# A four-layer graph network on one core: one transpose moved from TensorE to transfers and VectorE, and the last layer's side steps pinned to given units

## The chip, the cores and the metric

The kernel runs on one core of a Trainium2 chip. The engines are TensorE (PE, whose weight loads are listed as PEld), VectorE (DVE), ScalarE (ACT), GpSimd (POOL) and SyncE (SP), which here issues transfers between the device memory and SBUF. Each engine works through its own list of instructions in order and waits on semaphores. The metric is the device time of one execution in microseconds (us).

## The reference, cut to what matters

All values are float32. The input x holds 128 samples of 64 nodes with 256 features, and adj is one 64 by 64 adjacency matrix. Each of four layers adds a graph network's output to its input and normalises the result over the features.

```python
x = _layernorm(x + _L0_gnn_ref(x, adj, W, a))      # attention: softmax over masked scores, times x @ W
x = _layernorm(x + _L1_gnn_ref(x, ...))            # 4 heads, attention along 512 edges
x = _layernorm(x + _L2_gnn_ref(x, adj, ...))       # normalised adjacency, two linear maps, batch norms
x = _layernorm(x + _L3_gnn_ref(x, adj, ...))
...
def _L3_gnn_ref(x, adj, ...):
    h = relu(einsum('ts,bsh->bth', adj, x @ Wg0 + bg0))
    h = relu(einsum('ts,bsh->bth', adj, h @ Wg1 + bg1))
    for p in range(1, 5):                          # windows of p nodes through an LSTM
        nw = Tv // p
        wins = h[:, :nw * p, :].reshape(Bv * nw, p, Hd)
        last = _lstm_last(Wih[p - 1], Whh[p - 1], ..., wins)
        h = h.at[:, arange(nw) * p + (p - 1), :].set(last...)   # overwritten in place
    return h
```

So in the last layer every window length p reads what the one before has written.

## The kernel before, in words

**Recording.** A tile layer records the instructions, tracks which tile each reads and writes, and a scheduler then sets the order on every engine. `tc.issue_after(t)` makes what is recorded inside it stand behind instruction t on t's engine only; it adds no wait. A pool with `bufs=n` hands out n buffers in turn, and a new use waits for the last reader of the old one.

**Layers 0 and 1** go through the 8192 rows in 16 blocks called q, of 512 rows each, 128 on the partitions and four to a partition. For each q, `load_x` (L126) fetches the rows into `xin`; `l0_a` (L208) makes the transposed copy `tT` (features on the partitions) with `transposed` (L191): eight 128 by 128 TensorE transposes (L197) into two PSUM banks and two ScalarE copies (L198) out of them. `l0_b` multiplies it by the weights (L218), `l0_c` to `l0_e` do the attention, add the residual (L261) and write the normalised rows into `A[:, q, :]`. Layer 1 takes these, transposes them in the same way (`l1_t`), and `tT` has a single buffer that both use. The loop over q (its list of steps is at L649) interleaves: after each of eight `l1_graph` calls it runs the listed steps, among them `l0_e(q+1)` and `l0_a(q+2)` in the first slot and `l0_b(q+2)` in the third. `step` keeps TensorE's order as recorded; the other engines follow the scheduler. `load_x(q+2)` is called at the end of `l0_e(q)`. `A` has no other use for a q's columns before that, except that the setup keeps small tables in the columns at its upper end.

**The last layer** works on eight groups g of 16 samples. `lstm(g)` yields after each of 22 *units*: a unit computes the gates of one half (j) of the hidden state for one time step of one window length, with the input products on L970, the recurrent ones on L976, gate functions on L982 and L990, cell products on L985 to L989, and the new hidden state on L997 or L999. Units 0 to 3 belong to p=1, 4 to 7 to p=2, 8 to 13 to p=3, 14 to 21 to p=4. For p below 4 the last step overwrites `H` in place.

Between units, *side steps* are put in. `gcn(g, half)` makes the next group's H: it loads layer 2's residual (x2r), scales `A` (L879), transposes (by `turned`, in groups 1 to 7), adds (L884), normalises, then two graph products (L866, L909, L921, L866). `final(g, s)` transposes a quarter of the finished H, adds x3 (L1024), normalises and stores. `turned` (L844) is a transpose without TensorE: VectorE transposes squares of 32 (L848), one transfer writes the result to device memory (`way`, L851), four read it back with the squares in place (L853).

`steps_of(g)` gives the order of the 16 gcn steps of a group, and the loop hands them out evenly: after unit u, steps are run until done reaches (u+1)*16/20. `final(g, s)` runs whole after unit 14+2s, and the last one after unit 0 of the next group. Nothing there binds the order of ACT, DVE and POOL beyond the data.

```python
            while done < min(n_side, (u + 1) * n_side / (n_units - 2)):
                next(side, None)
                done += 1
```

Of the kernel before, what the change touches and what calls it, by code (L numbers as in the profile page):

```python
# [8 lines left out]
F32 = mybir.dt.float32  # L9
# [8 lines left out]
P = 128  # L18
NB = 128
N = 64  # L20
D = 256
KD = D // P
# [6 lines left out]
QT = 512  # L29
# [5 lines left out]
SKIP = 4  # L35
# [6 lines left out]
def kernel(ctx: ExitStack, tc: tile.TileContext, i, out):  # L42
    nc = tc.nc
# [68 lines left out]
    with ExitStack() as two:  # L112
# [13 lines left out]
        def load_x(q):  # L126
            xin[q] = xp.tile([P, PQ, D], F32, name="xin")
            nc.sync.dma_start(xin[q], x_view[q])

# [78 lines left out]
        def l0_a(q):  # L208
            L0[q] = {"x": xin.pop(q)}
            L0[q]["xT"] = transposed(L0[q]["x"], q)  # L210
# [611 lines left out]
    ST = 5  # L822
# [47 lines left out]
    def gcn(g, half, bank, name):  # L870

        q = g * 2 + half
        for a in range(2):
            x = work.tile([P, 2, D], F32, name="x2r", bufs=4)
            nc.sync.dma_start(x.rearrange("p c d -> p (c d)"), x2_dram[q][:, a * 2 * D:(a + 1) * 2 * D])
            blk = A[:, q, a * QT:(a + 1) * QT]
            z = blk.rearrange("p (c m t) -> p c m t", c=2, m=KD)
# [3 lines left out]
            if g:  # L881
                xt = turned(z.rearrange("p c m t -> p (c m) t"))
                xv = x.rearrange("p c (m i f) -> p c m i f", m=KD, f=32)
                nc.vector.tensor_add(xv, xt, xv)  # L884
            else:
                xt = bank([2, D])
                for m in range(KD):
                    for c in range(2):
                        nc.tensor.transpose(xt[:, c, m * P:(m + 1) * P], z[:, c, m, :], ident)
                nc.vector.tensor_add(x, xt, x)  # L890
            x3 = blk.rearrange("p (c d) -> p c d", c=2)
# [4 lines left out]
            yield  # L896
# [107 lines left out]
    def final(g, s, pieces=1):  # L1004
# [14 lines left out]
        o = work.tile([P, 2, D], F32, name="st", bufs=ST)  # L1019
        for cs in ([(0, 1)] if pieces == 1 else [(0,), (1,)]):  # L1020
            r = slice(cs[0], cs[-1] + 1)
            if pieces == 1:
                xv = xr.rearrange("p c (m i f) -> p c m i f", m=KD, f=32)
                nc.vector.tensor_add(xv, turned(h.rearrange("p c m t -> p (c m) t")), xv)  # L1024
            else:
                ht = gbank([2, D])
                for c in cs:
                    for k in range(KD):
                        nc.tensor.transpose(ht[:, c, k * P:(k + 1) * P], h[:, c, k], ident)
                nc.vector.tensor_add(xr[:, r], ht[:, r], xr[:, r])  # L1030
            layernorm(o[:, r], xr[:, r], len(cs), nc.gpsimd)
            for c in cs:
                nc.sync.dma_start(rows[1][c], o[:, c, :])

    def steps_of(g):

        if g:
            parts = [gcn(g, half, gbank, "hT") for half in range(2)]
            order = [0, 0, 1, 1] + [0] * (GCN_STEPS - 2) + [1] * (GCN_STEPS - 2)
        else:  # L1040
            parts = [gcn(g, 0, gbank, "hT"), gcn(g, 1, lbank, "hid")]
            order = [0, 0, 1, 1] + [0, 1] * (GCN_STEPS - 2)
        for half in order:
            next(parts[half])
            yield

    for _ in steps_of(0):
        pass
    n_units = sum(-(-(N // p) // (QT // GB)) * p * KD for p in range(1, SKIP + 1))
    first4 = n_units - SKIP * KD  # L1050
    for g in range(NG):

        side = steps_of(g + 1) if g + 1 < NG else iter(())
        n_side, done = 2 * GCN_STEPS, 0
        for u, _ in enumerate(lstm(g)):
            if u == 0 and g:
                final(g - 1, SKIP - 1)
            s, odd = divmod(u - first4, 2)
            if not odd and 0 <= s < SKIP - 1:
                final(g, s)  # L1060
            while done < min(n_side, (u + 1) * n_side / (n_units - 2)):
                next(side, None)
                done += 1
    final(NG - 1, SKIP - 1, pieces=2)
# [40 lines left out]
```

## Time and profile before

| | |
|---|---|
| median of 11 runs | 2175.81 us (2168.69 to 2177.08) |
| the profiled execution, its own time | 2176.67 us |
| its span, first to last instruction | 2174.9 us, mean granted TensorE clock 0.986 |
| PE / PEld busy | 2083.5 us (96%) / 1341.5 us (62%) |
| DVE / ACT / POOL busy | 863.4 us (40%) / 945.3 us (43%) / 415.8 us (19%) |
| transfers | 105.54 MB in 169275 packets, 86832 of them under 512 B |

Times in a view are counted from the start of the span. Layers 0 and 1 take about the first 560 us, layer 2 runs to about 850 us, and the last layer fills the rest. A row of a group of instructions reads: line, engine, operation, what is written and read, the shape, the count, then busy time and the mean of one, then the engine's idle time just before these instructions and what ended it. Matmuls overlap, so the time from one start to the next is the time that one costs; the printed duration is longer.

### The profile page before, as it was taken

How to read it: one execution, taken by the hardware profiler on the slowest of the kernel's cores; microseconds unless marked ns; L12 is line 12 of the kernel's file. 1: busy time of each engine (PE TensorE's matmuls, PEld its weight loads, DVE VectorE, ACT ScalarE, POOL GpSimd, SP SyncE). 2: the span in 40 equal slices, each digit the busy share in tenths (PEclk: the TensorE clock that was granted, in tenths of full speed). 3: DMA queues.
4: the chain of work that ended last, by engine and by line, in shares of the span. 5: the costliest groups of instructions: out<-in, count | busy, mean ns of one | idle time of the engine just before them, and what ended most of it. 6: DMA issues, size and time to landing. Idle time of an engine off the chain costs nothing.

```text
span 2174.9 us, 29437 instructions
## 1 busy us (share of the span) xinstructions
PE 2083.5 (96%) x11463; PEld 1341.5 (62%) x11463; DVE 863.4 (40%) x2054; ACT 945.3 (43%) x1825; POOL 415.8 (19%) x569
## 2 busy tenths in 40 slices
PE   6999999998999979999999999999999999999997
PEld 4667677775454434576576576477467468468466
DVE  7355655454544444134233333323323423423223
ACT  3766766674338153234234334333333333333332
POOL 1123333333210012011111111211211211202012
PEclk8999999999999989999999999999999999999999
DMA  3023222332221022012112111201201202201001
GB/s 124 20 42 52 45 49 50 53 51 42 42 86 59 0 87 78 0 47 67 42 35 63 58 30 58 69 21 52 85 10 59 87 6 60 72 1 59 20 7 52
DMA packets 169275, 105.54 MB, mean 49 GB/s; under 512 B 86832, under 2 KB 152368, under 8 KB 168880
## 3 DMA queue, kind: packets, MB, share of 16 engines
q1 hardware_dynamic: 167280, 101.70, 17.7%
q8 instruction: 90, 1.47, 0.3%
q0 software_dynamic: 1024, 1.05, 0.2%
q10 hardware_dynamic: 832, 0.92, 0.1%
q14 instruction: 49, 0.40, 0.1%
HBM read 59.59 MB, written 44.04 MB: 48 GB/s over the span
## 4 chain that ended last, share of the span: by engine, by line
PE 79%; DVE 7%; ACT 6%; DMA 3%; issue 2%; POOL 1%; SPq 1%; DVEq 0%; POOLq 0%; ACTq 0%
PE l L970 31%; PE l L976 19%; PE pz L707 5%; PE pz L772 4%; PE e L311 3%; PE g L909 2%; PE m L283 2%; PE g L921 2%; DMA way<-st 2%; PE m L218 2%; PE m L286 2%; PE g L866 1%; PE z L320 1%; PE m L401 1%; ACT A L879 1%
## 5 line engine op out<-in xcount | busy, mean ns | idle before, releaser
L970 PE MATMUL l<-H,wih 128*128 128x256 f32 (+2 forms) x2496 | 789.2, 471 | 9.9 <-ACT gate_g L990 4.4
L970 PEld LDWEIGHTS l<-H,wih 128*128 128x128 f32 x2496 | 469.9, 190 | 302.8 <-issue 189.2
L976 PE MATMUL l<-hid,whh 128*128 128x256 f32 (+2 forms) x1536 | 437.9, 438 | 2.4 <-DVE hid L999 2.4
L976 PEld LDWEIGHTS l<-hid,whh 128*128 128x128 f32 x1536 | 292.9, 191 | 131.7 <-issue 61.2
L982 ACT ACTIVATE gate_i<-l,bias 128x256 f32<-128x256 f32 (+2 forms) x176 | 100.0, 568 | 516.2 <-PE l L976 444.3
L985 DVE TENSOR_TENSOR gate_i<-gate_i,gate_g 128x256 f32<-128x256 f32 (+2 forms) x96 | 48.3, 503 | 432.8 <-ACT gate_g L982 432.7
L986 POOL TENSOR_TENSOR cell<-gate_f,cell 128x256 f32<-128x256 f32 (+2 forms) x96 | 84.5, 880 | 671.0 <-ACT gate_f L982 670.9
L83 POOL TENSOR_TENSOR ln_rs<-ln_rs,mhalf 128x2 f32<-128x2 f32 (+2 forms) x97 | 79.6, 821 | 688.0 <-DVE ln_rs L95 687.7
L322 ACT ACTIVATE u<-z 128x1024 f32<-128x1024 f32 x128 | 130.5, 1026 | 56.1 <-PE z L320 55.2
L982 ACT ACTIVATE gate_g<-l,bias 128x256 f32<-128x256 f32 (+2 forms) x176 | 100.2, 569 | 99.3 <-PE l L970 50.1
L990 ACT ACTIVATE gate_g<-cell 128x256 f32<-128x256 f32 (+2 forms) x176 | 90.0, 511 | 91.2 <-DVE cell L989 46.4
L982 ACT ACTIVATE gate_o<-l,bias 128x256 f32<-128x256 f32 (+2 forms) x176 | 99.2, 564 | 62.3 <-PE l L976 54.4
L707 PE MATMUL pz<-A,w 128*128 128x512 f32 x256 | 113.1, 595 | 0.0
L989 DVE TENSOR_TENSOR cell<-gate_i,gate_g 128x512 f32<-128x512 f32 (+2 forms) x80 | 49.9, 623 | 137.8 <-ACT gate_g L982 137.6
L294 DVE TENSOR_TENSOR qs<-m,qs 64x256 fp32r<-64x256 f32 x128 | 54.0, 422 | 121.8 <-ACT qs L293 120.1
L320 PE MATMUL z<-gath_r,qs 128*128 128x512 f32 x256 | 98.4, 472 | 0.0
L707 PEld LDWEIGHTS pz<-A,w 128*128 128x128 f32 x256 | 47.9, 190 | 55.3 <-issue 53.3
L283 PE MATMUL m<-wq,tT 128*128 128x260 f32 x256 | 72.5, 407 | 6.7 <-ACT yT L391 4.0
L982 ACT ACTIVATE gate_f<-l,bias 128x256 f32<-128x256 f32 (+2 forms) x96 | 51.0, 532 | 60.4 <-PE l L976 59.5
L999 DVE TENSOR_TENSOR hid<-gate_o,gate_g 128x256 f32<-128x256 f32 (+2 forms) x96 | 48.6, 507 | 67.8 <-ACT gate_g L990 39.8
L999 DVE TENSOR_TENSOR H<-gate_o,gate_g 128x512 f32<-128x512 f32 (+1 forms) x64 | 41.2, 643 | 80.3 <-PE l L970 68.0
L709 DVE BATCH_NORM_STATS2 st<-pz 128x6 f32<-128x512 f32 x64 | 44.4, 697 | 59.3 <-PE pz L707 59.2
(241 smaller groups left out, 2539.0 us busy)
## 6 DMA issues: line engine op xcount, KB each, us to landing
way<-st SPq DMA_DIRECT2D x59, 256.0 KB
st<-way SPq DMA_DIRECT2D x236, 64.0 KB
xin<-in_x SPq DMA_DIRECT2D x16, 512.0 KB
ld<-table SPq DMA_DIRECT2D x16, 512.0 KB
x_dram<-y SPq DMA_DIRECT2D x16, 512.0 KB
x2r<-x_dram SPq DMA_DIRECT2D x32, 256.0 KB
x_dram<-A SPq DMA_DIRECT2D x64, 128.0 KB
x3r<-x_dram SPq DMA_DIRECT2D x64, 128.0 KB
```

Of the source, the lines that this page charges most:

```text
L83: nc.gpsimd.tensor_tensor(dst, dst, mhalf[:, :n], OP.pow)
L283: nc.tensor.matmul(pq, xT[:, k, c * P:(c + 1) * P], wq[:, k, :], start=k == 0, stop=k == KD - 1)
L320: nc.tensor.matmul(z[:, k, :], L1[q]["qs"][c][:, s, k * P:(k + 1) * P], gath_r, start=True, stop=True)
L322: nc.scalar.activation(u, z, AF.Relu)
L707: nc.tensor.matmul(p_, w1[:, k, m * P:(m + 1) * P], A[:, q, k * QT:(k + 1) * QT], start=k == 0, stop=k == KD - 1)
L772: nc.tensor.matmul(p_, w2[:, k, m * P:(m + 1) * P], hidden(q, k), start=k == 0, stop=k == M1 - 1)
L970: nc.tensor.matmul(gates[n], wih[p][:, k, mw * P:(mw + 1) * P], Hw[:, k, :, s, :], start=k == 0, stop=not s and k == KD - 1)
L976: nc.tensor.matmul(gates[n], whh[p][:, k, m * P:(m + 1) * P], hid[:, k], start=False, stop=k == KD - 1)
L982: nc.scalar.activation(act[n], gates[n], AF.Tanh if n == "g" else AF.Sigmoid, bias=bias[:, p - 1, m:m + 1])
L986: nc.gpsimd.tensor_tensor(cell[:, j], act["f"], cell[:, j], OP.mult)
L990: nc.scalar.activation(act["g"], cell[:, j], AF.Tanh)
L999: nc.vector.tensor_mul(Hw[:, jj, :, s, :] if over else new[:, jj], o, t)
```

## The change

It has two parts.

**Layer 0.** For q from 1 on, `load_x` issues eight more transfers from SP. They read the same 512 rows again, and put 32 features' columns of every block of 32 rows on a quarter of the partitions, in pieces of 32 floats, into `A[:, q, :]`. `l0_a` then makes `tT` with one VectorE transpose of squares of 32 over 128 partitions by 1024 columns. The eight TensorE transposes and two ScalarE copies of these q are gone; q=0 is as before.

**Last layer.** `gcn`'s transposing half-steps are split for groups 1 to 7: two `fetch` steps (load, scale, turn) and two `norm` steps (add, normalise, store), so a half has ten steps. `final` is split at the turn's transfers into two steps, and takes its output tile only after the add. Each step is given a unit, in the tables AT and AT1 (a negative number counts back into the group before), in place of the even spread; steps on the same unit run with the later gcn steps first. All that a side step records on ACT, DVE and POOL stands behind the unit's last instruction there.

```diff
@@ load_x
             nc.sync.dma_start(xin[q], x_view[q])
+            if q:
+                rows = i["x"][q * QT:(q + 1) * QT, :].rearrange("(j t) (k i f) -> i k t j f", t=32, k=KD, f=32)
+                for n in range(4):
+                    for k in range(KD):
+                        to = A[n * 32:(n + 1) * 32, q, k * QT:(k + 1) * QT]
+                        nc.sync.dma_start(to.rearrange("t (j f) -> t j f", f=32), rows[n, k])
@@ l0_a
-            L0[q]["xT"] = transposed(L0[q]["x"], q)
+            if q:
+                L0[q]["xT"] = work.tile([P, KD, QT], F32, name="tT", bufs=1)
+                nc.vector.transpose(L0[q]["xT"].rearrange("p k t -> p (k t)"), A[:, q, :])
+            else:
+                L0[q]["xT"] = transposed(L0[q]["x"], q)
@@ gcn
-        for a in range(2):
+        def fetch(a):
             x = work.tile([P, 2, D], F32, name="x2r", bufs=4)
...
             if g:
-                xt = turned(z.rearrange("p c m t -> p (c m) t"))
...
+                return x, turned(z.rearrange("p c m t -> p (c m) t"))
...
+        def norm(a, x, xt):
+            xv = x.rearrange("p c (m i f) -> p c m i f", m=KD, f=32) if g else x
+            nc.vector.tensor_add(xv, xt, xv)
...
+        if g:
+            came = []
+            for a in range(2):
+                came.append(fetch(a))
+                yield
+            for a in range(2):
+                norm(a, *came[a])
+                yield
+        else:
+            for a in range(2):
+                norm(a, *fetch(a))
+                yield
@@ final
-        o = work.tile([P, 2, D], F32, name="st", bufs=ST)
...
+                ht = turned(h.rearrange("p c m t -> p (c m) t"))
+                yield
...
-                nc.vector.tensor_add(xv, turned(h.rearrange("p c m t -> p (c m) t")), xv)
+                nc.vector.tensor_add(xv, ht, xv)
...
+            o = work.tile([P, 2, D], F32, name="st", bufs=ST)
             layernorm(o[:, r], xr[:, r], len(cs), nc.gpsimd)
@@ the loop over groups
-    def steps_of(g):
...
+    AT = [[5, 5, 6, 6, 7, 9, 9, 13, 13, 15], [-7, -6, -4, -2, 1, 3, 3, 7, 7, 11]]
+    AT1 = [0, 0, 1, 2, 3, 5, 5, 7, 7, 11]
+    side = {}
+    for g in range(NG):
+        for half in range(2) if g else ():
+            part = gcn(g, half, gbank, "hT")
+            for n, u in enumerate(AT1 if half and g == 1 else AT[half]):
+                side.setdefault((g - 1) * n_units + u, []).append((n < 7, part))
+        for s in range(SKIP):
+            if g < NG - 1 or s < SKIP - 1:
+                part = final(g, s)
+                u = (g + 1) * n_units if s == SKIP - 1 else g * n_units + first4 + 2 * s
+                for v in (u, u + 1 + s // (SKIP - 1)):
+                    side.setdefault(v, []).append((True, part))
+    engines = (mybir.EngineType.Activation, mybir.EngineType.DVE, mybir.EngineType.Pool)
     for g in range(NG):
-        side = steps_of(g + 1) if g + 1 < NG else iter(())
-        n_side, done = 2 * GCN_STEPS, 0
         for u, _ in enumerate(lstm(g)):
-            if u == 0 and g:
-                final(g - 1, SKIP - 1)
...
+            traced = nc.cur_bb.bb.instructions
+            with ExitStack() as order:
+                for e in engines:
+                    order.enter_context(tc.issue_after([t for t in traced[-300:] if t.engine == e][-1]))
+                for _, part in sorted(side.pop(g * n_units + u, []), key=lambda t: t[0]):
+                    next(part)
```

## The prediction

> **What bounds the kernel now.** I read the busy table by stretches of time first, to see which engine each stage leans on, then the groups of instructions, then the chain of waits and the timeline around the places that the change touches. The busy table, in microseconds of each engine:
>
> ```profile
> core 0: us, PE busy (x) PEld busy (x) DVE busy (x) ACT busy (x) POOL busy (x), PEclk, DMA share, GB/s
> 300.00:400.00 100.00, 94.70 (x857) 68.24 (x855) 58.44 (x155) 66.37 (x146) 34.05 (x41) 1.00 0.28 53
> 1400.00:1600.00 200.00, 198.63 (x981) 129.67 (x980) 65.47 (x146) 70.64 (x129) 30.09 (x44) 1.00 0.14 43
> ```
>
> TensorE is nearly always busy in both stages, and VectorE, ScalarE and the transfers have room. So an edit pays if it takes TensorE work away (layer 0) or one of its few gaps (last layer). The groups concerned:
>
> ```profile
> L197 PE MATMUL m<-ident,xin 128*128 128x128 f32 x128 | 18.3, 288 | 8.0 <-DMA xin<-in_x 5.6 <-ACT spad L295 2.4
> L970 PE MATMUL l<-H,wih 128*128 128x512 f32 x770 | 338.2, 595 | 7.0 <-DVE H L999 3.7 <-ACT gate_g L990 3.4
> L976 PE MATMUL l<-hid,whh 128*128 128x256 f32 x768 | 175.5, 382 | 2.4 <-DVE hid L999 2.4
> ```
>
> The last two rows (between 860 and 2175 us) hold nearly all idle time of TensorE inside the LSTM: 9.4 us. The wait table counts 6 waits for H, 7 for gate_g and a single one for hid, so the first two recur once a group. Here is layer 0's place in the chain, and the group boundary from p=1 to p=2 on TensorE's and VectorE's timelines:
>
> ```profile
> 297.80 1.02 ACT u L322
> 298.83 0.03 issue
> 298.85 0.18 ACT spad L295
> 299.03 0.04 issue
> 299.07 1.09 PE m L197 x8
> 300.16 0.47 PE z L320 x2
> ```
> ```profile
> 1189.50 2.81 PE L970 MATMUL l<-H,wih 128*128 128x512 f32 x6 [0.48 <-ACT gate_g L990]
> 1192.88 1.55 PE L970 MATMUL l<-H,wih 128*128 128x512 f32 x3 [0.56 <-DVE H L999]
> ```
> ```profile
> 1188.67 0.68 DVE L999 TENSOR_TENSOR H<-gate_o,gate_g 128x512 f32<-128x512 f32 x1
> 1191.53 0.69 DVE L884 TENSOR_TENSOR x2r<-st,x2r 128x512 f32<-128x512 f32 x1 [2.18 <-DMA st<-way]
> 1192.13 0.69 DVE L999 TENSOR_TENSOR H<-gate_o,gate_g 128x512 f32<-128x512 f32 x1
> ```
>
> The eight transposes stand in the chain, behind a PSUM bank that ScalarE frees. At 1189 TensorE, with no side step in its list, waits for the first half of H; then VectorE's second H product stands behind an add (L884) whose transfer lands late, though its input was there by 1190. The end of the kernel has the same fault once, with a final's add in front:
>
> ```profile
> 2145.73 3.26 DMA st<-way
> 2149.12 0.70 DVE x3r L1024
> 2151.09 0.34 DVE gate_i L985
> 2152.48 0.44 DVE hid L999
> ```
>
> [...]the 512-column ones last 595 ns but start 429 ns apart, so I count starts. [...]the new ones have 128 B. The trace has their like: the table loads (ld<-table, 4096 pieces of 128 B each) took 21.7 ns a piece on one of 16 engines, against some 50 ns for 1024 B, so four times the cost per byte.[...] the turns here show 1.9 to 3.9 us. [...]the 128x512 transposes took 690 to 708 ns[...].
>
> **Layer 0, step by step.**
> *Removed:* 15 times eight transposes. Their starts are 109 ns apart, so 0.87 us for each q; also two ScalarE copies of 597 ns. In the chain above, the next matmuls (L320) could start when ScalarE's u is done, 298.83, instead of 300.16: 1.3 us. I take 1.0 us for each of the 14 q in the loop, 14.0 us, with ends 0.87 and 1.3.
> *Added on VectorE:* 15 transposes of 128x1024, which the trace lacks. [...]at most twice 708 ns, 1.42. In the changed order each stands between two of the qs subtractions (L294), just after the matmuls that release tT. There VectorE waits for ScalarE: L294 has 121.8 us of idle time before its 128 instructions. tT is then ready near 298, and its reader L218 comes at 303.85, or 302.5 without the transposes. So it costs nothing[...].
> *Added transfers:* 120 issues on SP. The xin issue takes 0.37 us, the ld ones with eight times as many pieces 0.5 to 3.1; at 0.4 to 0.5 that is up to 60 us of SP. 61440 pieces of 21.7 ns are 83 us of all 16 engines. Neither is near a limit: the order puts them right behind the xin loads, far ahead of use, most within the first 280 us, and the DMA share there goes from about 0.25 to about 0.55. Queued behind them on SP are the next xin, ld<-table and y stores. Each batch has eight transfers, 5.5 us, and the next ld waits for the scatters anyway. A late ld would hold POOL at L379, whose product L387 reads 11 us later (278.75 to 289.94). xin itself is now needed only for the residual.
> *q=1 in the setup:* its transpose comes behind L497 (23.77), so L218 starts near 26 instead of 23.52. ScalarE, which slowed L218 there, is free by then, and VectorE idles 4.04 us before L261: +0.5 us, between 0 and 2.5.
>
> **Last layer, step by step.** Matmuls, turns and adds are the same in number; they are moved.
> *p=1 to p=2:* the changed order puts the two L909 products (eight matmuls, 8 x 0.43 = 3.4 us) right after unit 3, and no x2r add there. TensorE now works while both H products are made (needed: 0.7 us for the first, some 2 for the second). Gone is, start to start, 1189.50 - (1184.56 + 10 x 0.429) = 0.65 and 1192.88 - (1189.50 + 6 x 0.429) = 0.81, about 0.73 over the groups. Groups 1 to 6: 6 x 1.38 = 8.3 us. Group 7 has no side step and keeps its 0.65.
> *The end:* the changed VectorE order puts the last final's add behind the hid product that it held up: 2.4 us gone. The add then waits in front of a unit about 13 us later than the turn, which takes about 9.
> *New waits:* half 0's adds stand at unit 6, one unit (13.7 us at p=2) behind the fetches; two turns on SP take about 15, but its VectorE products end 3 us after the unit. Its L866 comes 17 us after unit 6's end (unit 7 and the L921 products), the norms need about 8.5. Final's add stands one unit (2.6 us at p=4) behind its turn, and the next unit's gate product is queued behind it on VectorE; I work out the add at 13.4 us after unit 13's end, and that product at 16.4, so both fit. In group 0 half 1's two turns start at unit 0 and L866 stands after unit 3, 20.6 us on; I get its rows at about 23: +1 us against the 1.3 lost there now.
>
> **Sum.** -14.0 + 0.5 - 8.3 - 2.4 + 1.0 = -23.2 us. The profiled execution (span 2174.9, its own time 2176.67, so 1.8 around it) would be 2153.5; that run lies 0.86 above the median of 2175.81, which gives 2153 (2152.6).
>
> **Rivals.** A difference of 0.2%, 4.4 us, is about what can be told from none.
> - *The waits in the last layer only move* (the gap appears at unit 7 or at unit 14): for it, the pinned adds wait for transfers of 1.9 to 3.9 us, which vary; against it, the room above. 2175.8 - 13.5 = 2162.
> - *Layer 0 gives nothing*, because ScalarE or VectorE takes the place of TensorE: for it, the chain between 287.7 and 292.8 runs through ScalarE; against it, the edit frees ScalarE of 1.2 us at the very place. 2175.8 - 9.7 = 2166.
> - *The change doesn't do what it says*: the scheduler had these steps in as good places, and gains and losses cancel, 2176. Against it: the new list has L909 where the gap was.
> - *Slower:* pinned final adds wait in VectorE's list for their turn, and the gate product behind them delays hid. There are 3 such finals in each of 8 groups, 24, with 3 us of room on VectorE and, as hid is wanted a unit and a half later, about 6 on TensorE. Only past 6 us does it cost; at 7.5 us lateness it takes 24 x 1.5 = 36 us, minus 23: 2189. Against it: turns would have to take 16 us, not 9.
>
> **How the numbers follow.** Forecast 0.60 (own range 2145 to 2160), last layer nothing 0.13, layer 0 nothing 0.08, no effect 0.07, slower 0.12. So faster 0.81, same 0.07, slower 0.12. Low end: 15 x 1.3 + 8.3 + 2.4 = 30, with 2 us to spare, 2143. High end 2174: it takes in both half cases and part of the case without effect.
>
> **What would show it.** No L197 row on xin but 8 matmuls; [...]the period of two q, now 63.64 us (209.74 to 273.39 at L218), near 61.6; the L970 idle of 7.0 us down to about 0.5 and the L976 idle of 2.4 gone. It is wrong if L218 waits for VectorE, if VectorE's transposes wait for A's transfers, or if L866 or L976 show idle time in every group.

## The result, and the profile after

The changed kernel takes 2138.90 us, median of 8 runs (2138.42 to 2140.98), against 2174.74 us for the kernel before (31 runs). The ratio is 0.9838, 95% interval 0.9830 to 0.9847: 1.6% faster, some 36 us. The prediction said 2153, with a range of 2143 to 2174. So the direction was right, but the gain was half as large again as the sum, and the time lies 4 us below the low end.

Where it went is read from the starts of TensorE's instructions in the two traces, stage by stage (a pz product is one of layer 2's). The spans differ by 37.3 us (2174.9 to 2137.6). The lines of the changed kernel that are named here are 7 to 25 higher than before, but for those up to L97, which are the same: L218 is now L230, L879 is L890, L909 is L933, L970 is L994, L976 is L1000, L999 is L1023.

| stage, start to start | before | after | difference | in the prediction's sum |
|---|---|---|---|---|
| first matmul to first pz product (layers 0 and 1) | 535.4 | 518.4 | -17.0 | -13.5 |
| first to last pz product (layer 2) | 248.3 | 248.3 | 0 | 0 |
| last pz product to first unit (group 0's graph steps) | 42.1 | 36.2 | -5.9 | nothing |
| first group of units | 168.5 | 168.6 | +0.1 | +1.0 |
| groups 1 to 6 | 1011.5 | 1001.1 | -10.4 | -8.3 |
| group 7 to the last product of the LSTM | 153.1 | 148.8 | -4.3 | -2.4 |

Every row but layer 2's is off in the same direction, and one of them the prediction didn't have at all. First the busy table of the changed kernel, in the two stages in which the prediction showed it before:

```profile
core 0: us, PE busy (x) PEld busy (x) DVE busy (x) ACT busy (x) POOL busy (x), PEclk, DMA share, GB/s
284.00:384.00 100.00, 94.91 (x848) 68.65 (x847) 66.44 (x165) 65.47 (x146) 35.96 (x40) 1.00 0.29 53
1363.00:1563.00 200.00, 200.00 (x973) 128.37 (x972) 69.27 (x154) 73.33 (x134) 35.33 (x49) 1.00 0.15 48
```

In the last layer TensorE now has no idle time left in this stretch (200.00 of 200, before 198.63). In layers 0 and 1 its share hardly moved; the work became less and the same share of a shorter time. The groups, with the different shapes kept apart:

```profile
L994 PE MATMUL l<-H,wih 128*128 128x512 f32 x832 | 363.6, 593 | 1.8 <-ACT H L957 1.2 <-ACT gate_g L1014 0.5
...
L1000 PE MATMUL l<-hid,whh 128*128 128x256 f32 x768 | 173.6, 379 | 0.0
...
L220 DVE STREAM_TRANSPOSE tT<-A 128x1024 f32<-128x1024 f32 x15 | 18.7, 1245 | 0.4
...
L204 PE MATMUL m<-ident,xin 128*128 128x128 f32 x8 | 1.9, 424 | 5.7 <-DMA xin<-in_x 5.7
```

Eight transposes of xin are left, VectorE's new transpose takes 1.25 us (the prediction's bound was 1.42), and it has 0.4 us of idle time in front of it over all 15: it never waits for the new transfers. The waits in front of the LSTM's products went from 7.0 and 2.4 us to 1.8 and 0.0; 1.2 of the 1.8 stand in front of group 0's first product, outside the stretch in which the 7.0 were counted, so that like for like 0.5 and 0.0 are left, as forecast. This is the boundary from p=1 to p=2 in a middle group, on TensorE's and on VectorE's timeline (two fences):

```profile
1161.68 4.45 PE L994 MATMUL l<-H,wih 128*128 128x512 f32 x10
1165.98 3.60 PE L933 MATMUL g<-hT,wg 128*128 128x512 f32 x8
1169.41 9.18 PE L994 MATMUL l<-H,wih 128*128 128x512 f32 x21
```
```profile
1165.79 0.68 DVE L1023 TENSOR_TENSOR H<-gate_o,gate_g 128x512 f32<-128x512 f32 x1
1167.14 0.69 DVE L1023 TENSOR_TENSOR H<-gate_o,gate_g 128x512 f32<-128x512 f32 x1 [0.67 <-ACT gate_o L1006]
```

Both H products are done by 1167.83, while TensorE still works on L933 until 1169.4: no idle time stands in brackets behind the TensorE lines, as forecast.

The row that the prediction didn't have is group 0's. These are ScalarE's and TensorE's timelines ahead of its first L909 product, in the kernel **before**:

```profile
779.01 31.55 ACT L879 ACTIVATE A<-A,sh,sc 128x256 f32<-128x256 f32 x64 [64.63 <-DVE sh L692]
810.47 0.57 ACT L903 ACTIVATE hT<-g 128x512 f32<-128x512 f32 x1
```
```profile
805.86 1.24 PE L866 MATMUL l<-bdT,A 64*64 64x64 f32 x32 [0.61 <-POOL A L97]
811.09 3.78 PE L909 MATMUL g<-hT,wg 128*128 128x512 f32 x4 [3.98 <-ACT hT L903]
```

and here the same place **after**:

```profile
777.07 2.08 ACT L890 ACTIVATE A<-A,sh,sc 128x256 f32<-128x256 f32 x4 [12.78 <-DVE sh L704]
786.58 0.60 ACT L927 ACTIVATE hT<-g 128x512 f32<-128x512 f32 x1 [7.44 <-PE g L878]
```
```profile
788.97 1.25 PE L878 MATMUL l<-bdT,A 64*64 64x64 f32 x32 [0.62 <-POOL A L97]
790.14 3.22 PE L933 MATMUL g<-hT,wg 128*128 128x512 f32 x4
```

Before, ScalarE ran all 64 shifts L879, those of all eight groups, in one block of 31.6 us, and only then the copy of hT that group 0's first L909 product needs. TensorE stood still for 3.98 us. After, eight shifts run there (two blocks of four) and the others at their units, and TensorE has no wait. The page of the kernel before had the hint: its chain of waits by line ends with "ACT A L879 1%", and 1% of the span is 22 us.

### The profile page after: what moved, and what is told of

The parts are those of the page before. It is cut to its first block, busy times and chain, and to the rows that moved or that the text cites. A ratio compares the mean times of both kernels' runs of the same rounds, so it can differ in the third digit from the quotient of the medians.

```text
span 2137.6 us, 29441 instructions
## 1 busy us (share of the span) xinstructions
PE 2062.0 (96%) x11343; PEld 1330.6 (62%) x11343; DVE 888.1 (42%) x2069; ACT 932.4 (44%) x1795; POOL 429.8 (20%) x569
## 3 DMA queue, kind: packets, MB, share of 16 engines
q0 software_dynamic: 1024, 1.05, 0.2%
## 4 chain that ended last, share of the span: by engine, by line
PE 87%; DVE 6%; ACT 3%; issue 1%; DMA 1%; POOL 1%; SPq 0%; ACTq 0%; POOLq 0%; DVEq 0%
PE l L994 36%; PE l L1000 20%; PE pz L784 5%; PE pz L719 5%; PE e L323 3%; PE g L933 2%; PE m L295 2%; PE g L945 2%; PE m L298 2%; PE z L332 2%; PE m L230 2%; PE g L878 1%; PE m L413 1%; PE m L270 1%; DVE ln_st L92 1%
## 5 line engine op out<-in xcount | busy, mean ns | idle before, releaser
L994 PE MATMUL l<-H,wih 128*128 128x256 f32 (+2 forms) x2496 | 787.5, 470 | 1.8 <-ACT H L957 1.2
L994 PEld LDWEIGHTS l<-H,wih 128*128 128x128 f32 x2496 | 471.4, 190 | 286.2 <-issue 185.6
L1000 PE MATMUL l<-hid,whh 128*128 128x256 f32 (+2 forms) x1536 | 435.9, 437 | 0.0
L1000 PEld LDWEIGHTS l<-hid,whh 128*128 128x128 f32 x1536 | 291.8, 190 | 128.4 <-issue 61.2
L1023 DVE TENSOR_TENSOR hid<-gate_o,gate_g 128x256 f32<-128x256 f32 (+2 forms) x96 | 47.4, 494 | 61.3 <-ACT gate_o L1006 35.0
L1023 DVE TENSOR_TENSOR H<-gate_o,gate_g 128x512 f32<-128x512 f32 (+1 forms) x64 | 41.3, 645 | 66.6 <-PE l L994 46.2
```

The costliest lines, as they stand in the source:

```text
L994: nc.tensor.matmul(gates[n], wih[p][:, k, mw * P:(mw + 1) * P], Hw[:, k, :, s, :], start=k == 0, stop=not s and k == KD - 1)
L1000: nc.tensor.matmul(gates[n], whh[p][:, k, m * P:(m + 1) * P], hid[:, k], start=False, stop=k == KD - 1)
L1023: nc.vector.tensor_mul(Hw[:, jj, :, s, :] if over else new[:, jj], o, t)
```

## The experiments

### Each part alone

`l0_only` is the kernel before with the change's `load_x` and `l0_a`; `ll_only` is the changed kernel with those two as before. The lines in question, as `l0_only` adds them:

```diff
             nc.sync.dma_start(xin[q], x_view[q])
+            if q:
...
+                        nc.sync.dma_start(to.rearrange("t (j f) -> t j f", f=32), rows[n, k])
...
-            L0[q]["xT"] = transposed(L0[q]["x"], q)
+            if q:
+                L0[q]["xT"] = work.tile([P, KD, QT], F32, name="tT", bufs=1)
+                nc.vector.transpose(L0[q]["xT"].rearrange("p k t -> p (k t)"), A[:, q, :])
+            else:
+                L0[q]["xT"] = transposed(L0[q]["x"], q)
```

> Layer 0's part alone, the last layer as before. The prediction's own sum for it was -13.5 us. The two traces put the start of the next stage (L707 before, L719 after) 16.5 us earlier, 1.24 us for each q in the steady loop (0.87 of matmuls and some 0.35 of waiting for the bank) and more in the first four q. Theory A (the parts are independent, the loop's price was low): 2158 to 2160. Theory B (layer 0's gain is 13.5 as forecast, the rest of it is later work that only starts sooner): 2161 to 2163. Theory C (part of the last layer's gain comes from layer 0's transposes freeing buffers or SP): under 2156.

> The last layer's part alone, layer 0 as before. Forecast by the prediction: -9.7 us, 2166. By the traces, counted from the start of L707 or L719 to the end: -20.5, so 2155 (2153 to 2156) if the parts are independent. In the trace there should be no wait of the first L933 product (before: 3.98 us on hT), none of 0.65 us between p=1 and p=2 in groups 1 to 6, and none of 2.4 us at L1000.

Measured: 2157.41 us (ratio 0.9920, 0.9904 to 0.9935) and 2154.61 us (0.9910, 0.9895 to 0.9926), against 2175.05. That is 17.4 and 19.6 us by the ratios, 17.6 and 20.4 by the medians; their sum, 37 to 38, is the change's own gain within these intervals. So the parts add up (theory A). By stages, layer 0's part takes layers 0 and 1 from 535.4 to 517.3 us; the last layer's part alone has 36.2, 168.6, 1001.1 and 148.8 us in the four last rows of the table, to the tenth those of the changed kernel. Both forecasts (13.5 and 9.7) were too small, the second was half of what came. The old last layer itself is less steady: in `l0_only`'s trace its four rows are 42.5, 167.5, 1015.6 and 149.8 us, against 42.1, 168.5, 1011.5 and 153.1 in the kernel before.

### Group 0: is it ScalarE's block?

`act_pin` adds one thing to the kernel before, ScalarE's pin; `no_act_pin` takes that one thing from the changed kernel.

```diff
+            traced = nc.cur_bb.bb.instructions
+            last = [t for t in traced[-300:] if t.engine == mybir.EngineType.Activation][-1]
+            with tc.issue_after(last):
                 while done < min(n_side, (u + 1) * n_side / (n_units - 2)):
                     next(side, None)
```
```diff
-    engines = (mybir.EngineType.Activation, mybir.EngineType.DVE, mybir.EngineType.Pool)
+    engines = (mybir.EngineType.DVE, mybir.EngineType.Pool)
```

> The kernel before, with one thing of the change: ScalarE's part of the gcn side steps may not be issued ahead of the unit after which it stands in the program. So only 8 of the 64 shifts L879 stand in front of the first L903 copy, instead of all 64 (64 x 0.49 = 31 us of ScalarE). Theory S (those 64 hold the hT copy, so TensorE waits 3.98 us at L909 and runs at half its clock for longer): group 0 gives 5.2 to 5.8 us, L909 has no wait; the first stall between p=1 and p=2 (0.65 us) stays in groups 1 to 6 and the second may go where the H products come ahead of the adds, up to 5 us; total 2165 to 2170. Rival R (group 0's gain comes from where half 1's products stand, not from ScalarE): 2174 to 2176.

> The changed kernel with the issue order pinned on VectorE and GpSimd only; ScalarE's side steps are free again, and all 64 shifts stand in one block ahead of the first hT copy. Theory S: the wait of about 4 us at the first L933 product and its half-rate matmuls come back, 5 to 6 us: 2144 to 2145. Rival R: 2139 to 2140. Should the free ScalarE order also bring back waits between p=1 and p=2, they would show at L994.

Measured: `act_pin` 2168.02 us, ratio 0.9967 (0.9957 to 0.9977), 7 us faster. Its stage from the last pz product to the first unit takes 36.4 us, not 42.1. TensorE's timeline of `act_pin`:

```profile
807.98 1.24 PE L866 MATMUL l<-bdT,A 64*64 64x64 f32 x32 [0.62 <-POOL A L97]
809.15 3.33 PE L909 MATMUL g<-hT,wg 128*128 128x512 f32 x4
```

The wait is gone with nothing else of the change in place; the waits between p=1 and p=2 are still there (6.4 us in all in front of L970). `no_act_pin` took 2140.93 us, only 2 above the changed kernel, though its trace had the wait back and 41.4 us for the stage; it happened to have a shorter layer 0 (512.8 us) in the profiled execution. So it was run again.

> The run with ScalarE's order free, once more. Its first run had the wait of 4.17 us at L933 back (from the last pz product to the first unit 41.4 us instead of 36.2), but its median was only 2 us above that of the changed kernel, as the profiled execution spent 5.6 us less before the first L719. Layer 0 is the same instruction for instruction. Theory N (this is scatter of layer 0's stretches at half the clock): layer 0 takes 515 to 519 us from first matmul to first pz this time, total 2141 to 2145. Theory M (something outside the last layer differs): 512 to 514 again, 2140 to 2141.

Measured: 2144.30 us, 5.4 above the changed kernel, with layer 0 at 517.1 us (theory N). ScalarE's and TensorE's timelines of this second run:

```profile
761.09 31.55 ACT L890 ACTIVATE A<-A,sh,sc 128x256 f32<-128x256 f32 x64 [64.64 <-DVE sh L704]
792.54 0.57 ACT L927 ACTIVATE hT<-g 128x512 f32<-128x512 f32 x1
```
```profile
787.86 1.24 PE L878 MATMUL l<-bdT,A 64*64 64x64 f32 x32 [0.61 <-POOL A L97]
793.16 3.78 PE L933 MATMUL g<-hT,wg 128*128 128x512 f32 x4 [4.06 <-ACT hT L927]
```

Added or taken away alone, the pin on ScalarE moves this stage by 5.2 to 5.7 us, both ways. Some 4 us of that are the wait; the rest is mainly that more of the L909 products behind it run at half the clock (five lose 0.42 us each in the kernel before, three after). Rival R is out.

### The boundary from p=1 to p=2: the filling or the order on VectorE?

`no_pins` keeps the new units but pins nothing:

```diff
-    engines = (mybir.EngineType.Activation, mybir.EngineType.DVE, mybir.EngineType.Pool)
+    engines = ()
```

> The changed kernel without any pinned issue order: the side steps are called at the same units, but every engine may issue them when the scheduler likes. TensorE's list is the same but for one place in group 0: the L933 products stand between p=1 and p=2. VectorE has the x2r adds (L902) ahead of the second H product again. Theory F (the L933 products fill the gap, whatever VectorE's order): no wait between p=1 and p=2; the 64 shifts of ScalarE come back in one block before L927 (4 us of waiting, 5 us in all): 2141 to 2144. Theory V (the order on VectorE is what removes the second wait): 0.7 us of idle time again in groups 1 to 6, 4 to 5 us more: 2146 to 2149.

Measured: 2146.01 us. The number falls between the two theories, and the trace decides. TensorE's and VectorE's timelines of `no_pins` at the same boundary:

```profile
1170.48 3.60 PE L933 MATMUL g<-hT,wg 128*128 128x512 f32 x8
1173.91 14.47 PE L994 MATMUL l<-H,wih 128*128 128x512 f32 x33
```
```profile
1170.29 0.69 DVE L1023 TENSOR_TENSOR H<-gate_o,gate_g 128x512 f32<-128x512 f32 x1
1173.01 0.69 DVE L902 TENSOR_TENSOR x2r<-st,x2r 128x512 f32<-128x512 f32 x1 [2.03 <-DMA st<-way]
...
1174.08 0.68 DVE L1023 TENSOR_TENSOR H<-gate_o,gate_g 128x512 f32<-128x512 f32 x1
```

The fault that the prediction named is back on VectorE: the second H product stands behind an add that waits 2.03 us for its transfer, and is done at 1174.76. It costs nothing, because with L933 in front TensorE needs it only six products after 1173.91, near 1176.5. So the eight L933 products remove both waits by themselves (theory F), and the seven microseconds against the changed kernel are mainly group 0's graph steps (42.3 instead of 36.2 us) and 0.8 at the end; groups 1 to 6 lose 1.4 in this trace, and the first group gains 1.6.

### The end of the kernel

`tail_back` issues the last group's first three finals as before, whole at their unit and unpinned:

```diff
-            if g < NG - 1 or s < SKIP - 1:
+            if g < NG - 1:
...
+            s, odd = divmod(u - first4, 2)
+            if g == NG - 1 and not odd and 0 <= s < SKIP - 1:
+                for _ in final(g, s):
+                    pass
```

> The changed kernel with the three finals of the last group (s = 0 to 2) issued whole at their unit and outside the pinned order, as before; VectorE's list at the end is then that of the kernel before, with the add (L1049) of the last of them ahead of the hid product. In the kernel before this place cost 2.41 us of waiting at L976 and 1.8 us of matmuls at half the clock, in the 3.4 us that followed. Theory T1 (the add in front of the product is the cause, and the wait brings the half clock with it): up to 4.3 us, 2141 to 2143.5, an idle time at L1000 of up to 2.4 us; in the run with layer 0's part alone and in that with ScalarE pinned alone the same add cost 0.72 and 0.48 us with no half clock after it, so it may be as low as 0.5. Rival T2 (the tail's gain comes from elsewhere in the last group): 2139, no idle time at L1000.

Measured: 2140.67 us; the last stage takes 149.6 instead of 148.8 us, with a wait of 0.59 us in front of L1000. The place is right (T1), but its price is a matter of when the transfer lands. In the seven traces that keep the old last layer or pin ScalarE alone in it, the wait is between 0.48 us (`act_pin`) and 2.68 (`copy_twice_c`). The kernel before had a long one:

```profile
2152.96 4.97 PE L976 MATMUL l<-hid,whh 128*128 128x256 f32 x14 [2.41 <-DVE hid L999]
```

and `tail_back` a short one:

```profile
2118.56 3.29 PE L1000 MATMUL l<-hid,whh 128*128 128x256 f32 x14 [0.59 <-DVE hid L1023]
```

The same 14 products took 4.97 us after the long wait and 3.29 after the short one. After the long one the granted clock was at one half for about 3.4 us (0.58, 0.50 and 0.91 in three slices of 1.7 us from 2153.6), which makes 1.7 us more. After the 0.59 us of `tail_back` the clock stayed at 1.00. The last stage took 153.1 and 153.4 us in the two traces with a wait above 2 us, and 149.5 to 150.4 in the five others, so that the usual gain at this place is 0.7 to 1.6 us and not the 4.3 of the table.

### Layer 0: what is its gain made of?

Four runs on parts of the step. `xin_twice`, `copy_twice_c` and `both_twice_c` add once more, in the kernel before, what the change removes; `loads_only` has the new transfers alone.

The first line pair is in `xin_twice` and `both_twice_c`, the second in `copy_twice_c` and `both_twice_c`, for q of 1 to 15 (`times` and `copies` are 2 there); `loads_only` has the `load_x` lines of `l0_only`.

```diff
-                for c in range(PQ):
+                for c in list(range(PQ)) * times:
                     nc.tensor.transpose(p_[:, c, :], src[:, c, k * P:(k + 1) * P], ident)
-                nc.scalar.activation(t[:, k, :], p_.rearrange("p c t -> p (c t)"), AF.Copy)
+                for _ in range(copies):
+                    nc.scalar.activation(t[:, k, :], p_.rearrange("p c t -> p (c t)"), AF.Copy)
```

> The kernel before with the eight TensorE transposes of xin (L197) done twice for q of 1 to 15; the second time writes the same values over the first, and ScalarE's copies stay as they are. This prices the TensorE part of what the change removes. Theory P1 (TensorE sets the pace there, so a transpose is worth its start spacing of 0.109 us): 15 x 0.87 = 13 us, 2188. Theory P2 (the wait for ScalarE's bank sets the pace, the transposes lie beside it): 2175 to 2178, and then the 17 us that layer 0's part gave alone are ScalarE's.

> The kernel before with ScalarE's two copies (L198, 0.6 us each) of the transposed xin done twice for q of 1 to 15. Theory Q1 (ScalarE's copies set the pace beside TensorE there, each is worth its full time): 15 x 1.2 = 18 us, 2193. Theory Q2 (they are worth what the change's 1.19 us a q leaves over TensorE's 0.75 to 0.87, so 0.3 to 0.45 us a q): 5 to 7 us, 2180 to 2182. Theory Q3 (ScalarE has room): 2175.

> The kernel before with both the TensorE transposes and ScalarE's copies of xin done twice for q of 1 to 15: what the change removes, added once more. If the price is the same on both sides, 1.19 us a q, so 17 to 18 us: 2192. If ScalarE's and TensorE's parts add fully, 15 x (0.87 + 1.2) = 31 us: 2206. If only TensorE counts: 2178 as in the run with the transposes alone.

> The kernel before with the 120 new transfers of 128-byte pieces and nothing else: what they load is not used, and layer 0 still transposes on TensorE. Prediction's step (hidden: neither SP nor the 16 engines are near a limit): 2173 to 2177. Rival (the transfers delay the table loads, the y stores or the setup): up to 15 us more, 2180 to 2190; then layer 0's gain without them would be as much larger.

| run | median, us | ratio to before (interval) | per q, q = 7 to 15, against before |
|---|---|---|---|
| xin_twice | 2177.93 | 1.0017 (1.0010 to 1.0023) | +0.73 |
| copy_twice_c | 2175.00 | 0.9999 (0.9989 to 1.0008) | +0.2, all of it in one q |
| both_twice_c | 2182.40 | 1.0035 (1.0023 to 1.0047) | +0.71 |
| loads_only | 2177.81 | 1.0015 (1.0009 to 1.0022) | 0.0 |
| the change | 2138.90 | 0.9838 (0.9830 to 0.9847) | -1.19 |

The last column is worked out from the starts of L218 (or its like) for q = 7 and 15, 254.6 us apart in the kernel before and 245.1 after. ScalarE's copies have room (Q3): doubled they cost nothing. TensorE's transposes are worth 0.73 of their 0.87 us in the steady loop (P1), and with both doubled it is again 0.71, so only TensorE counts. The change gains more than that, 1.19, because it also takes away what TensorE lost around them: start to start, the products of the transposes' line (L197, then L204) lost 9.9 us beyond their own spacing between q = 7 and q = 15 before, and 7.2 after, 0.34 for each q. Doubling the transposes doesn't double that wait, so the mirror image is cheaper than the removal; that last step is an argument from the traces, no run isolates it. `xin_twice` costs less in all (3.2 us, which alone would have pointed to P2) than 15 x 0.73 = 11, since up to q = 5 it is ahead of the kernel before: there it has none of the stretches at half the clock which the kernel before has near 92 and 126 us.

The transfers alone cost 3 us by the medians, and the interval leaves zero out (2 to 5 us), where the prediction had nothing. Layers 0 and 1 don't show it (533.6 us, against 535.4). The trace does show a place in the last layer: groups 1 to 6 take 1016.1 us instead of 1011.5, because the second wait at p=1 to p=2 is 1.79 us long in group 1 and 2.40 in group 4, the latter with 3.4 us at half the clock behind it. `l0_only`, the other run with the new transfers and the old last layer, has the same (1.52 and 2.10 us, 1015.6); the five other traces with these waits have 1010.9 to 1012.0. In the last layer each engine's instructions stand in the same order as in the kernel before; why these turns then land later stays open. In the changed kernel these waits are gone.

Three more runs change one thing in the changed kernel: `l0_late` uses the new path for q of 4 and more only, `turn_twice` issues VectorE's transpose twice, `loads_twice_c` each new transfer twice.

The three edits in this order (the first in `load_x` and in `l0_a`):

```diff
-            if q:
+            if q > 3:
...
                 nc.vector.transpose(L0[q]["xT"].rearrange("p k t -> p (k t)"), A[:, q, :])
+                nc.vector.transpose(L0[q]["xT"].rearrange("p k t -> p (k t)"), A[:, q, :])
...
                         nc.sync.dma_start(to.rearrange("t (j f) -> t j f", f=32), rows[n, k])
+                        nc.sync.dma_start(to.rearrange("t (j f) -> t j f", f=32), rows[n, k])
```

> The changed kernel with layer 0's part for q of 4 to 15 only: q = 1 to 3 load and transpose as before (24 TensorE transposes and six copies of ScalarE come back, 24 transfers go). Per q the steady loop showed 1.24 us, so 3.7 us for three: 2142.5. Theory E1 (the first q gain more because there ScalarE and the setup are in the way; the traces put q = 1 to 4 at 6.0 us): up to 2145. Theory E2 (the first q gain nothing of their own, the new loads are in the way of the setup): 2139 or less.

> The changed kernel with every VectorE transpose of layer 0 issued twice, one after the other, into the same tile: 15 x about 1.3 us more on VectorE. Prediction's step (VectorE has cover there, the transpose costs nothing): 2138.5 to 2140. Rival (the transpose stands on the path through the qs subtractions to TensorE): 15 x 1.3 = 20 us, 2158; half covered, 2149.

> The changed kernel with each of the 120 new transfers issued twice, so another 61440 pieces of 128 bytes and another 83 us of the 16 engines by 21.7 ns a piece. Prediction's step (hidden): 2138 to 2141. Rival (each set costs the 3 us that the loads alone cost in the kernel before): 2142; if SP or the engines become the limit in the first 280 us, more, 2145 to 2160.

Measured: 2140.52, 2166.09 and 2205.22 us. The first is 1.6 us above the changed kernel by the medians and 4.2 by the profiled executions' layer 0 (522.6 against 518.4): the early q are worth something between the two, with 3.6 as the price of three others, and the run is too coarse to tell E1 from E2.

The second is a miss: +27 us, more than the 20 of full cost. VectorE's timeline of `turn_twice` shows why, and then TensorE's:

```profile
304.19 1.25 DVE L220 STREAM_TRANSPOSE tT<-A 128x1024 f32<-128x1024 f32 x1
305.47 0.42 DVE L307 TENSOR_TENSOR qs<-m,qs 64x256 fp32r<-64x256 f32 x1
...
309.03 1.21 DVE L221 STREAM_TRANSPOSE tT<-A 128x1024 f32<-128x1024 f32 x1
```
```profile
310.39 3.73 PE L231 MATMUL m<-w,tT 128*128 128x258 f32 x16 [0.31 <-DVE ln_mv L93]
```

The first copy stands between two qs subtractions, where it was free. The second was given another slot, in a run of VectorE work (305.5 to 324) that holds layer 0's norm and then layer 1's softmax scans, and the reader L231 starts at its heels (309.03 + 1.21 = 310.24). There each 1.25 us lies on the path: 1.8 us a q in the steady loop, which includes one more stretch at half the clock (about 3.4 us long) every second q from 257 to 455 us. So VectorE's cover depends on the slot, not on its average of 66%. The chain of waits of the changed kernel says the same; part of it between 289 and 304 us:

```profile
289.20 1.07 PE e L342 x2
290.27 0.02 issue
290.30 0.70 DVE e L344
...
302.47 0.14 DVE ln_mv L93
302.61 0.01 issue
302.61 0.66 PE m L241 x4
```

From 290.3 to 302.6 the chain runs on VectorE, but for one activation of 0.64 us on ScalarE and 2.7 us listed as issue.

The third, +66 us, has the same cause by another way. In `loads_twice_c` the scheduler put VectorE's transpose behind the softmax scans, at 264.40, and TensorE waited for it:

```profile
256.39 1.03 PE L333 MATMUL z<-gath_r,qs 128*128 128x512 f32 x2
265.76 6.10 PE L231 MATMUL m<-w,tT 128*128 128x258 f32 x16 [8.34 <-DVE tT L221]
```

There are nine such waits, 61.5 us together. VectorE itself waited for a transfer once, 3.1 us. So it was not the transfers that were late, but the place of the transpose in VectorE's order. That no transpose waits for the single set of loads follows from the changed kernel's trace (0.4 us in front of all 15); whether they cost something elsewhere, this run can't tell.

### The half clock in layer 0

`fill` repeats the four transposes of e (L366) four times more, in all eight softmax groups (the expectation says four by mistake); `fill_two` only in the two behind which TensorE waits for dn, a result of VectorE's scans. The repeated ones write the same values. The edit of `fill_two` (in `fill` the condition is `row is e` alone):

```diff
                     nc.tensor.transpose(p_[:, c, :], row[:, c * P:(c + 1) * P], ident)
+                if row is e and S in (0, 6):
+                    for c in range(4 * EC):
+                        nc.tensor.transpose(p_[:, c % EC, :], row[:, c % EC * P:(c % EC + 1) * P], ident)
```

> The changed kernel with 16 more TensorE transposes of 0.109 us behind each of the four groups m<-ident,e of L366, which write the same values once more. They fill 1.7 of the 2.1 to 2.4 us in which TensorE waits there for dn. After two of these waits (120 and 482 us in the changed kernel) the granted clock is one half for 6 us. Theory C1 (the half clock follows a wait of about 2 us): both stretches at half clock are gone from the records, 1.7 us each gained where TensorE sets the pace: 2134 to 2137. Theory C2 (the half clock does not follow this wait): the stretches stay, 2139, or up to 2 us more if the extra transposes delay dn.

> The changed kernel with the 16 repeated transposes only in the two softmax groups behind which TensorE waits for dn (S = 0 near 120 us and S = 6 near 482 us). With the filling in all eight groups the time to the first pz product was 515.9 us instead of 518.4, though each of the five groups between cost about 0.55 us. Theory C1 (each stretch at half the clock costs what its matmuls lose, 1.7 to 2 us for 6.8 us): 513 to 515 us to the first pz product, total 2134 to 2137. Theory C3 (layer 0 is bound by VectorE there, the half clock is hidden): 2138.5 to 2140.

> The changed kernel once more, unchanged, beside the run with two fillings: 2138 to 2141.

Measured: `fill` 2139.87, `fill_two` 2135.82, `after_again` 2138.30 us. The busy table of the changed kernel around the two waits, where PEclk (the third number from the end) is the granted clock, and then that of `fill_two`:

```profile
118.00:128.00 10.00, 7.24 (x36) 4.18 (x34) 7.17 (x13) 5.22 (x9) 2.18 (x2) 0.66 0.59 117
480.00:490.00 10.00, 7.37 (x33) 3.82 (x34) 6.25 (x18) 2.22 (x3) 4.03 (x6) 0.66 0.01 3
```
```profile
118.00:128.00 10.00, 8.92 (x56) 5.92 (x54) 6.49 (x16) 5.88 (x17) 2.18 (x2) 1.00 0.64 129
480.00:490.00 10.00, 9.31 (x153) 6.43 (x155) 5.70 (x18) 5.50 (x12) 5.21 (x7) 1.00 0.16 58
```

With the waits filled the clock stays at 1.00 in both places, as it does in `fill`: the half clock follows the wait (C1). It costs time: from the first L230 of q=15 to the first pz product the changed kernel takes 79.1 us, `after_again` 78.6 and `fill_two` 75.9, and all three have one more stretch at half the clock near 511 to 517 us. The whole of layers 0 and 1 can't show the gain: it takes 512.7 us in `fill_two` and 518.4 in `after_again`, but 512.8 also in `no_act_pin`, where neither wait is filled. By the medians the gain is 2.5 us, with ranges that overlap (2134.76 to 2138.54 and 2135.96 to 2139.88), so `fill_two` is ahead of the changed kernel by a margin too small to be sure of. In `fill` the other six groups took it back: 515.9 us for layers 0 and 1, and 251.5 instead of 248.3 for layer 2.

## Why the prediction was right and wrong, point by point

**Layer 0, removed work: right mechanism, term too small.** The prediction took 1.0 us a q from ends of 0.87 and 1.3, for 14 q. Measured in the steady loop: 1.19 a q, the period of two q 61.3 us (forecast 61.6). 15 x 1.19 = 17.9 explains the 17.0 us of the stage in the changed kernel and the 18.0 in `l0_only`. The chain had shown 1.3 directly, and the middle value was a choice.

**Layer 0, added work: right for the place where it stands.** The transpose takes 1.25 us, under the bound of 1.42 that the prediction worked out from the 128x512 ones (708 ns), waits for no transfer, and in the loop delays nothing that the trace shows. The prediction named the cover, VectorE's idle time in front of L294 (121.8 us in all before 128 instructions); the transposes are 15 x 1.25 = 19 us in all. The reason given, that VectorE has room, was too broad: `turn_twice` lost 27 us a slot further on. The step for q = 1 held: L230 there starts at 24.30, behind the end of the transpose at 24.24, and so 0.8 us later than L218 before (forecast 0.5, between 0 and 2.5), and it is made up by q = 2.

**Layer 0, added transfers: hidden in the loop, and cheaper than forecast.** The DMA share of the first 280 us went from 0.27 to 0.44, not to 0.55: the estimate took the table loads' 21.7 ns for each piece of 128 bytes, and most new pieces took about 13. (By its own figures such a piece cost 3.5 times as much per byte as one of 1024, not four times.) What the transfers did outside layer 0 is the 3 us of `loads_only`.

**Last layer, "matmuls, turns and adds are the same in number; they are moved": the step that failed.** It followed the moved steps on TensorE, VectorE and SP, and left out what `gcn` issues on ScalarE: eight shifts a group, 64 in all, which nothing bound to their units before. Their block stood in front of group 0's hT copy. Taking them out of it is worth 5.2 to 5.7 us, as the two pin runs show; the prediction had nothing. It had looked for the new waits of the pins, and not for the old waits that pinning ends. This is the largest part of the 14 us by which the sum fell short; layer 0 makes 3.5 of it, p=1 to p=2 2.1, the end 1.9 and group 0's units 0.9. With the shifts free again the changed kernel took 2140.93 and 2144.30 us.

**Group 0's +1.0: a slip in the sum, beside a wait that is not usual.** The wait of about 1 us inside unit 4 came (0.54 us listed as idle, about 1 us in all), and the 1.3 us before it went, as written; the text set one against the other, and the sum counted only the loss. The stage came out at +0.1. But those 1.3 us (1.05 of waiting for gate_g in front of L970) are in the kernel before's trace alone: in the six other traces with the old units the stage takes 167.5 to 167.7 us, and against these the change does cost 1.0.

**p=1 to p=2: right, 8.3 forecast and 10.4 measured.** Against the other traces with the old units it is 9.7 to 15.0. Beside the two waits, the products right behind each lost another 0.07 to 0.1 us, and the second wait was longer in two groups (1.05 and 0.85 us). `no_pins` shows that the filling does it. What the prediction said of VectorE's add was true of the timeline and immaterial.

**The end: right place, 2.4 forecast and 4.3 measured.** The wait was counted, the half clock behind it was not. Both figures come from a trace in which this wait happened to be long; that 2.4 lies between the usual 0.7 to 1.6 us and these 4.3 is luck. In that stretch of 3.41 us the 128x256 products start 427 ns apart instead of 216; after how much idle time such stretches came is counted in the last section.

**The rivals.** None came. The pinned adds do wait for their turns (70.9 us in all in front of 24 L1049, at most 4.5 in front of one), but no gate product behind them is late on TensorE. The low end of 2143 was too high because it took in the upper price of the terms counted and left no room for a term that was forgotten.

## What to carry to other kernels

When a change pins or moves steps, list every engine on which they issue, and look for the place where the old, free order let them stand in front of something urgent: here the work that depended on nothing late had been hoisted furthest, and one line of 1% in the chain of waits may be all that shows it. A share of busy time says nothing on whether one more instruction is free; the same 1.25 us cost nothing in one slot of VectorE's list and all of it, and more, in another (1.8 us a q in `turn_twice`). A wait of two microseconds on TensorE is to be priced with the slower products that can follow it (here 1.7 us more after 2.41 us of waiting), and a wait at which other matmuls already exist is best filled with them, as eight L933 products did at p=1 to p=2. And a wait on a transfer that is seen once in one trace is no price: here the same one lasted 0.5 us in one run's trace and 2.7 in another's.

## What the runs showed of the hardware that was not expected

After some waits of 2 us and more TensorE's granted clock was one half for 3.4 or 6.8 us, and 128x256 products started 427 ns apart instead of 216. The length of the wait alone doesn't tell these waits from the others. In each of the 19 traces the stretches at half the clock start on a grid of 3.413 us, and they go with TensorE's idle time within one step of that grid. Taken over all traces from 60 us on, for steps at the full clock, with the ends of matmuls as the profile models them: after a step with more than 1.80 us of idle time the clock fell every time (72 of 72), after one with less than 1.48 us never (0 of 11268), between the two in 20 of 60; the kernel before and the changed kernel alone have 10 of 10, 0 of 1184 and 1 of 6. Here are the steps around one wait for dn, first in the kernel **before** (wait of 1.96 us up to 126.38, all in one step), then in `xin_twice` (1.95 us up to 124.69, cut by a line of the grid):

```profile
122.95:126.36 3.41, 1.34 (x7) 0.63 (x7) 2.55 (x3) 3.25 (x6) 0.00 (x0) 1.00 0.36 129
126.36:129.78 3.42, 2.72 (x12) 2.33 (x13) 2.24 (x4) 0.99 (x2) 0.00 (x0) 0.50 0.00 0
```
```profile
120.51:123.93 3.42, 2.23 (x12) 1.55 (x10) 2.65 (x4) 2.51 (x5) 0.00 (x0) 1.00 0.22 79
123.93:127.34 3.41, 1.89 (x14) 1.45 (x15) 2.56 (x3) 1.93 (x4) 0.00 (x0) 1.00 0.00 0
127.34:130.75 3.41, 3.41 (x25) 1.55 (x25) 3.08 (x10) 1.65 (x3) 1.23 (x1) 1.00 0.03 10
```

Several short waits in one step did it too: in `ll_only` 0.58, 0.69 and 0.45 us between 246.98 and 250.39 left TensorE 1.70 us busy of 3.41, and the next step ran at half the clock. A single wait of 0.5 to 0.9 us, as in the last layer, never did: in the kernel before the clock is 1.00 from 815.9 to 2153.9 us, with all those of p=1 to p=2 in between. Filling a wait with 16 repeated transposes kept the clock at 1.00 in both places tried. The grid lies differently against the program from one execution to the next (a stretch starts at 120.24 us in the changed kernel's trace and at 124.26 in `after_again`'s, 4.02 us apart and so not whole steps), which fits that such stretches fall differently in the same instructions: layers 0 and 1 of the changed kernel's code took 512.8 us in one profiled execution and 517.1 to 518.8 in five others.
